# One stream of attention across eight images: second layer behind the next image's first unit, four single PSUM banks for the maxima

## The chip, the cores and the metric

The kernel runs on one core of a Trainium2 chip. A core has five engines with instruction queues of their own: TensorE (PE in the profile; its weight loads are PEld), VectorE (DVE), ScalarE (ACT), GpSimd (POOL) and SyncE (SP, which here only issues DMAs). Each engine takes its instructions in the order in which the program gives them; an instruction whose inputs are not ready holds up all that stand behind it on that engine. Matmul results land in PSUM, which has eight banks of 2 KB per partition (512 fp32 columns on 128 partitions). The metric is the device time of one execution in microseconds (us).

## What is computed

The input is eight images of 32 x 32 positions and 256 channels (1024 tokens of 256). Cut to what matters, the reference is

```python
x = x + L0_conv(group_norm(x))          # layer 0: 3x3 convolution and attention side by side
t = tokens(x)
t = t + L1_attn(layer_norm(t))          # layer 1: plain attention
t = t + L1_ffn(layer_norm(t))           # two experts per image
```

with, in layer 0,

```python
conv_out = conv3x3(x, conv_w) + conv_b                      # 192 channels
k, q, v = split(x @ qkv_w + qkv_b); q = q * DKH ** -0.5     # 64 each, 8 heads of 8
logits = q @ k.T + rel_w + rel_h                            # 1024 x 1024 for each head
attn = softmax(logits) @ v                                  # 64 channels
out = concat([conv_out, attn @ attn_w + attn_b])
```

where `rel_w` and `rel_h` are products of q with tables of relative positions. Layer 1 is attention with one head of 128 over the 1024 tokens (`softmax(Q @ K.T / sqrt(128)) @ V @ W_o + b_o`, plus its input). The feed-forward part chooses two of eight experts per image from the mean token, and stands behind all eight images.

## The kernel before

Layer 0's attention of an image is cut into four *units*. A unit is one half of the queries (512) and four of the eight heads. For a unit the kernel holds a tile `F` (queries together with the relative-position features, 128 partitions, for both halves of the keys) and a tile `KM` (keys together with 0/1 rows that pick the positions), so that one matmul of `F` with `KM` gives the whole logit. `KM` has one copy, used by the even units in heads 0 to 3 and by the odd ones in heads 4 to 7.

Each unit goes through two passes, because the maximum over the keys has to be known before the exponential:

- *score* (`Unit.score`): for 128 queries and one head, two matmuls of 512 keys into a PSUM tile of two banks (L610), and one DVE maximum over its 1024 columns (L617). 16 of these make a unit. PSUM holds two such tiles (`ps_lg`), and nearly all other small PSUM work goes through the same two.
- *fold* (`Unit.fold`): the 16 maxima are split into two fp32r parts, turned by four transposes (L628), copied to a row (L634), and written by four small DMAs on SP's queue into rows of `F` (L636), so that the next matmul gives the logit less its maximum.
- *weigh* (`Unit.weigh`): the transposed logit for 128 keys and one head, 512 columns (L646), and its exponential on ACT (L653). 32 of these make a unit.
- *gather* (`Unit.gather`): for each 128 keys, eight matmuls of the weights with the values (L661), four of them at a time side by side in the array. After the last, ACT copies the sum and *settle* turns and divides it.

The order of the work is written out by hand (`tc.manual_schedule()`); no planner moves anything. `first_layer` runs an image's four units in steps. A step `s` scores two heads of unit `s // 8` and weighs four heads of the unit that lies ten steps (`lead = NT + LAG`) behind:

```python
lead = NT + LAG
for s in range(units[0].scored // 2, NU * NT + lead + 1):
    u, j = divmod(s, NT)
    w, k = divmod(s - lead, NT)
```

So at first steps only score, then score and weigh, and the last ten only weigh. Between them `fill.send(us)` puts in other work: one step of a *chain* (generators that stop at each `yield`: `normalise` of the next image from step 12 on, `project`, `token_mean`), and `us` worth of *dense* work (the convolution's matmuls, L550, in pieces of estimated cost 0.36 us).

`normalise` transposes the next image (L339), takes group statistics (L349), makes q, k and v, writes the keys to DRAM, and combines the image on DVE (L433) and POOL (L436) into the six tiles `V` of the convolution. `queries` and `keys` load `F`'s source and `KM` (L490) by DMA, `features` makes the relative-position parts (L506) and writes them to DRAM, from where `Unit.__init__` loads `F` (L591, L595).

When an image's weighing has ended, `first_layer` issues `keys` of the next image, ends the second `project` half, and `second_layer` follows: for each 128 tokens two score matmuls (L846), one maximum over 1024 columns (L849), one exponential over 1024 columns (L852), transposes (L864), and for each 256 tokens the product with the values (L929) and with `W_o` (L940). Beside it run the pieces of `features` and the first scores of the next image's unit 0. `token_mean` stores the image and takes its mean for the expert choice.

## Time and profile before

| | us |
|---|---|
| median of three runs | 2888.73 (2887.54 to 2895.56) |
| profiled execution | 2892.55 |
| its span, first to last instruction | 2890.8 |
| PE busy | 2432.7 |
| DVE busy | 1408.4 |
| ACT busy | 975.7 |
| POOL busy | 369.8 |
| mean granted TensorE clock | 0.92 of full speed |

How to read it: the page gives busy time by engine over one execution, 40 slices of the span with busy tenths, the chain of work that ended last, and groups of equal instructions (line, engine, operation, output<-inputs, shapes, count | busy us, mean ns of one | idle time of the engine just before them and what ended it). A row of a table of windows is one stretch: its length, then for each engine busy us and the number of instructions, then the granted TensorE clock, the busy share of the 16 DMA engines and GB/s. A row of the timeline is start, length, engine, line, operation and tiles, with the idle time of the engine before it in brackets. SPq is SyncE's sequencer issuing DMAs.

In the span, image 2's second layer begins at 903.3 us, and image 3's at 1190.0 us; image 0's first score stands at 123.2, the last image's second layer runs from 2298.1 to 2344.5, and the feed-forward part follows.

### The profile page before, as it was taken

The page shows a single profiled execution, that of the slowest core. Times are in us where ns is not written, and L with a number is a line of the kernel's source. Part 1 is how long each engine was busy: PE and PEld are TensorE (multiplying, and loading weights), DVE is VectorE, ACT ScalarE, POOL GpSimd, SP SyncE. Part 2 cuts the span into 40 slices and gives each one's busy share as a digit, 9 for nine tenths or more (in the row PEclk, how much of TensorE's full clock was granted, in tenths as well). Part 3 has the DMA queues.
Part 4 walks back from the last instruction along what each step waited for, and adds up shares of the span by engine and source line. Part 5 has one row for each costly group of instructions (what it writes and reads, how often), then busy time and mean ns, then how long its engine had stood idle before and what let it go on. Part 6 is the DMA issues. An engine that isn't in the chain of part 4 may idle for free.

```text
span 2890.8 us, 28135 instructions
## 1 busy us (share of the span) xinstructions
PE 2432.7 (84%) x10731; PEld 1466.5 (51%) x10731; DVE 1408.4 (49%) x2525; ACT 975.7 (34%) x1717; POOL 369.8 (13%) x290
## 2 busy tenths in 40 slices
PE   4678878887898788878987888788889769999998
PEld 3544545455445544544454445544554346666665
DVE  6456356536643564366436644663467242332232
ACT  1035313531453145314531453145225422223222
POOL 3111102100211021102110211021100021111110
PEclk6789988998899899989998999899989979999999
DMA  3530343034213411441144114411421031112110
GB/s 94 128 76 18 76 105 64 22 78 104 53 31 84 102 40 31 87 103 37 31 87 102 37 31 97 92 38 34 112 59 31 1 106 58 59 59 73 58 51 22
DMA packets 81945, 185.94 MB, mean 64 GB/s; under 512 B 8546, under 2 KB 20715, under 8 KB 79507
## 3 DMA queue, kind: packets, MB, share of 16 engines
q1 hardware_dynamic: 79154, 182.05, 26.4%
q10 hardware_dynamic: 2656, 2.10, 0.3%
q8 instruction: 85, 1.39, 0.2%
q14 instruction: 50, 0.40, 0.1%
HBM read 112.15 MB, written 62.52 MB: 60 GB/s over the span
## 4 chain that ended last, share of the span: by engine, by line
PE 68%; DVE 20%; ACT 6%; issue 3%; DMA 2%; POOL 1%; SPq 1%; ACTq 0%; DVEq 0%; POOLq 0%
PE st L646 9%; PE po L661 8%; PE py L1214 8%; PE phd L1196 8%; DVE mx L617 7%; PE lg L610 6%; PE pc L550 5%; PE po L929 4%; PE lg L846 3%; PE pq L745 2%; ACT PT L653 2%; PE pmean L971 2%; DVE nm L849 2%; DVE V L433 2%; PE pk L386 2%
## 5 line engine op out<-in xcount | busy, mean ns | idle before, releaser
L653 ACT ACTIVATE PT<-st 128x512 f32<-128x512 f32 x1024 | 590.5, 597 | 492.1 <-PE st L646 444.9
L617 DVE TENSOR_REDUCE mx<-lg 128x1 f32<-128x1024 f32 x512 | 605.1, 1216 | 237.7 <-PE lg L610 235.1
L610 PE MATMUL lg<-KM,F 128*128 128x512 f32 x1024 | 379.7, 457 | 147.9 <-DVE mx L617 54.7
L646 PE MATMUL st<-F,KM 128*128 128x512 f32 x1024 | 470.2, 479 | 32.8 <-ACT PT L653 28.7
L646 PEld LDWEIGHTS st<-F,KM 128*128 128x128 f32 x1024 | 192.5, 197 | 340.0 <-ACT PT L653 258.4
L550 PE MATMUL pc<-convw,V 128*128 128x192 f32 x1152 | 296.5, 363 | 47.1 <-POOL V L436 29.2
L610 PEld LDWEIGHTS lg<-KM,F 128*128 128x128 f32 x1024 | 195.3, 206 | 244.1 <-DVE mx L617 92.1
L661 PE MATMUL po<-PT,vk 128*32 128x512 f32 x2048 | 292.4, 632 | 0.0
L550 PEld LDWEIGHTS pc<-convw,V 128*128 128x128 f32 x1152 | 216.4, 209 | 89.9 <-POOL V L436 32.7
L1214 PE MATMUL py<-w,hT 128*128 128x256 f32 x1024 | 237.3, 385 | 0.0
L1196 PE MATMUL phd<-n2T,w 128*128 128x512 f32 x512 | 223.2, 594 | 0.0
L1214 PEld LDWEIGHTS py<-w,hT 128*128 128x128 f32 x1024 | 189.9, 190 | 45.6 <-issue 22.4
L1221 DVE TENSOR_TENSOR r<-py,n 128x256 f32<-128x256 f32 x64 | 27.1, 424 | 311.2 <-PE py L1214 311.2
L846 PE MATMUL lg<-nqk 128*128 128x512 f32 x256 | 141.0, 679 | 24.1 <-ACT pr L852 24.1
L1196 PEld LDWEIGHTS phd<-n2T,w 128*128 128x128 f32 x512 | 97.0, 191 | 115.8 <-issue 108.9
L852 ACT ACTIVATE pr<-lg,nm 128x1024 f32<-128x1024 f32 x64 | 71.3, 1113 | 217.2 <-DVE nm L850 202.8
L733 POOL TENSOR_TENSOR T<-T,n 128x256 f32<-128x256 f32 x64 | 48.3, 773 | 717.8 <-DVE n L730 717.8
L567 DVE TENSOR_TENSOR ms<-mm 128x192 f32<-128x192 f32 x32 | 11.4, 357 | 239.5 <-ACT mm L565 239.5
L1203 ACT ACTIVATE hT<-phd,b1c 128x512 f32<-128x512 f32 x128 | 86.3, 686 | 97.6 <-PE phd L1196 97.4
L379 POOL TENSOR_TENSOR T<-T,l0b 128x2048 f32<-128x2048 f32 x8 | 36.2, 4527 | 643.8 <-PE tpx L339 643.8
L849 DVE TENSOR_REDUCE nm<-lg 128x1 f32<-128x1024 f32 x64 | 78.1, 1220 | 80.6 <-PE lg L846 80.6
L929 PE MATMUL po<-pt,v 128*128 128x256 f32 x512 | 115.9, 379 | 0.4 <-DVE pt L867 0.4
(246 smaller groups left out, 2525.0 us busy)
## 6 DMA issues: line engine op xcount, KB each, us to landing
F<-fd SPq DMA_DIRECT2D x64, 768.0 KB
fy<-rel SPq DMA_DIRECT2D x32, 512.0 KB
F<-fy SPq DMA_DIRECT2D x128, 128.0 KB
w<-in_L_ffn_W_dram SPq DMA_DIRECT2D x32, 512.0 KB
T<-in_x_dram SPq DMA_DIRECT2D x16, 512.0 KB
scr<-kqh SPq DMA_DIRECT2D x64, 128.0 KB
fd<-kqh SPq DMA_DIRECT2D x32, 256.0 KB
KM<-kd SPq DMA_DIRECT2D x32, 256.0 KB
```

The lines of the kernel that those rows point to most:

```text
L550: nc.tensor.matmul(pc[:, i], lhsT=V[j][:, kc, (16 * g + dy) * NQ : (16 * g + dy) * NQ + P], rhs=convw[:, j, dy * KC + kc], start=dy + kc == 0,
L610: nc.tensor.matmul(lg[:, a, :], lhsT=self.F[:, a, hl, i * P : (i + 1) * P], rhs=KM[:, self.g * HG + hl, a * 512 : (a + 1) * 512], start=Tr ...
L617: nc.vector.tensor_reduce(self.mx[:, i, hl : hl + 1], lg.rearrange("p a s -> p (a s)"), AX.X, ALU.max, negate=True)
L646: nc.tensor.matmul(st, lhsT=KM[:, self.g * HG + hl, j * P : (j + 1) * P], rhs=self.F[:, j // 4, hl, :], start=True, stop=True,)
L653: nc.scalar.activation(self.pts[j][:, hl, :], st, AF.Exp)
L661: nc.tensor.matmul(self.po[32 * hl : 32 * hl + 32, :], lhsT=vk[:, j, (self.g * HG + hl) * (DH + 1) : (self.g * HG + hl) * (DH + 1) + 32], ...
L846: nc.tensor.matmul(lg[:, h, :], lhsT=q, rhs=k[:, h * 512 : (h + 1) * 512], start=True, stop=True)
L849: nc.vector.tensor_reduce(nm, lg, AX.X, ALU.max, negate=True)
L929: nc.tensor.matmul(po[:, 0:IB], lhsT=sec.v[:, jc, :], rhs=pt[:, jc, :], start=jc == 0, stop=jc == NT - 1)
L1196: nc.tensor.matmul(phd, lhsT=ws[k][0][:, kc, f * P : (f + 1) * P], rhs=n2T[:, kc, q * 512 : (q + 1) * 512], start=kc == 0, stop=kc == KC - 1,)
L1203: nc.scalar.activation(hT[:, k * NF + f, :], phd, AF.Gelu, bias=b1c[:, f, k * B + b : k * B + b + 1])
L1214: nc.tensor.matmul(py, lhsT=hT[:, k * NF + f, j * P : (j + 1) * P], rhs=ws[k][1][:, f, :], start=False, stop=k == TOPK - 1 and f == NF - 1,)
```

## The change

The four parts of it:

1. `ps_lg` becomes four single banks instead of two pairs. A *score* is now one matmul of 512 keys and one DVE maximum over 512 columns, 32 to a unit; `fold` takes the smaller of the two negated halves first. The second layer's scores, maxima and exponentials go by halves too, and its value product uses a bank of this pool.
2. `first_layer` runs over 32 steps an image, without a lag: each step weighs four heads of its unit, and beside them scores the *next* unit, also across images (the next one of image b's unit 3 is image b+1's unit 0). Scores stand at places 3 to 27 of a unit's 32 weighing places, `fold` (DVE) at place 28, `fold_in` (transposes, row, DMAs) at place 30.
3. An image's second layer, with both halves of its projection, moves into the next image's run: `project` is chained during the next image's unit 0, and `second_layer` stands whole between the next image's units 0 and 1. The last image's follows at the end, alone.
4. All filling goes in smaller pieces and at every weighing place (`normalise`, `combine`, `features`, `project`), `features` and `queries` become part of the chain of `normalise`, the next image's tile is fetched at step 8, `keys` is loaded in two halves of four heads each, and `F` has three fixed places instead of a ring of three.

The diff, cut to its core ("..." marks what is left out):

```diff
-        ps_lg = ph.enter_context(tc.tile_pool(name="ps_lg", bufs=2, space=PSUM))
+        ps_lg = ph.enter_context(tc.tile_pool(name="ps_lg", bufs=4, space=PSUM))
...
-            return ps_lg.tile([P, 2, 512], FP, tag="lg", name=name)
+            return ps_lg.tile([P, 512], FP, tag="lg", name=name)
...
-        def f_tile(name, dt=FR):
-            return work.tile([P, 2, HG, 512], dt, tag="F", name=name, bufs=3)
+        def f_tile(name, place, dt=FR):
+            return work.tile([P, 2, HG, 512], dt, tag=f"F{place}", name=name)
...
             for kc in range(KC):
-                tp = turned(kc)
-                for q in range(2):
-                    nc.vector.bn_stats(st[:, kc, q, :], tp[:, q, :])
+                for g in range(2):
+                    nc.vector.bn_stats(st[:, kc, g, :], turned(kc, g))
+                    yield None
...
+            while b > 0 and (done[b - 1] < NT or not may_query.get(b)):
+                yield None
+            qs, qx = queries(b)
...
-            while b > 0 and done[b - 1] < NT:
-                yield None
             yield from combine(b, base)
-
+            yield from features(b, qs, qx)
+            yield None
+            yield None
+            yield None
+            units[b, 0] = Unit(b, 0)
+            yield None
...
-        def keys(b):
+        def keys(b, g):
+            hs = slice(g * HG, (g + 1) * HG)
             for i in range(4):
                 nc.sync.dma_start(
-                    out=KMb[8 * i : 8 * i + 8], in_=kds[b % 2][i % 2].rearrange("(d h) s -> d h s", h=NH)
+                    out=KMb[8 * i : 8 * i + 8, hs],
+                    in_=kds[b % 2][i % 2].rearrange("(d h) s -> d h s", h=NH)[:, hs],
                 )
...
-                self.F = f_tile("F")
+                self.F = f_tile("F", 2 if n == 3 else (b + n) % 2)
...
             def score(self):
 
-                i, hl = divmod(self.scored, HG)
+                n, a = divmod(self.scored, 2)
+                i, hl = divmod(n, HG)
                 self.scored += 1
                 lg = lg_tile("lg")
-                for a in range(2):
-                    nc.tensor.matmul(
...
+                nc.tensor.matmul(
+                    lg,
+                    lhsT=self.F[:, a, hl, i * P : (i + 1) * P],
+                    rhs=KM[:, self.g * HG + hl, a * 512 : (a + 1) * 512],
+                    start=True,
+                    stop=True,
                 )
+                nc.vector.tensor_reduce(self.mx[:, a, i, hl : hl + 1], lg, AX.X, ALU.max, negate=True)
 
             def fold(self):
 
+                assert self.scored == 32
+                m = self.mx[:, 0]
+                nc.vector.tensor_tensor(m, m, self.mx[:, 1], ALU.min)
...
+            def fold_in(self):
+
+                pm = lg_tile("pmx")
...
-        def first_layer(b, units):
...
-                if s == 12 and more:
-                    T[b + 1] = load_image(b + 1)
-                    fill.chains.append(normalise(b + 1))
...
+        def fetch(b):
+            T[b] = load_image(b)
+            for _ in range(4):
+                yield None
+
+        def pace(b, s, p):
+
+            if done.get(b, NT) < NT:
+                left, later = 4 * (15 - s) - p, 5.0 if s < NT else 0.0
+            else:
+                left, later = 4 * (32 - s) - p + 24, 5.0
+            return max(fill.owed - later, 0.0) / max(left, 1)
...
+        def first_layer(b):
+
             more = b + 1 < B
+            for s in range(NU * NT):
+                n, j = divmod(s, NT)
+                unit = units[b, n]
+                nxt = (b, n + 1) if n + 1 < NU else (b + 1, 0) if more else None
+                if s == 0:
+                    if b > 0:
+                        keys(b, 1)
+                elif s == NT:
+                    units[b, 2] = Unit(b, 2)
+                    if b > 0:
+                        while fill.chains:
+                            fill.send(0.4)
+                        second_layer(b - 1, sec, [units[b, 0].gather, lambda: settle(b, 0)], units[b, 2])
+                        fill.chains.append(token_mean(b - 1))
+                    else:
+                        units[b, 0].gather()
                         fill.send(0.4)
+                        settle(b, 0)
+                    if more:
+                        fill.chains.append(fetch(b + 1))
+                        fill.chains.append(normalise(b + 1))
+                elif s == NT + 1:
+                    units[b, 3] = Unit(b, 3)
+                elif s == 2 * NT:
+                    may_query[b + 1] = True
+                elif s == 3 * NT and more:
+                    keys(b + 1, 0)
+                    units[b + 1, 1] = Unit(b + 1, 1)
+                for p in range(HG):
+                    place = 4 * j + p
+                    unit.weigh(j, p)
+                    if nxt in units:
+                        u = units[nxt]
+                        while u.scored < min(32, (place - 3) * 4 // 3 + 1):
+                            u.score()
+                        if place == 28:
+                            u.fold()
+                        elif place == 30:
+                            u.fold_in()
+                    elif nxt is not None:
+                        assert place < 28
+                    if p == 1:
+                        if j > 0:
+                            unit.gather()
...
+                    if s == 1 and p == 0 and b > 0:
+                        sec = Second(b - 1)
+                        for half in range(2):
+                            fill.chains.append(project(b - 1, sec, half, (2, 4, 2)))
+                    fill.send(pace(b, s, p) * (0.6 if p == 1 else 1.13))
...
             def scores(self, blk, i, q, k, rs, scale):
-                lg = lg_tile("lg1")
+                lg = [lg_tile("lg1") for h in range(2)]
...
+                    nc.tensor.matmul(lg[h], lhsT=q, rhs=k[:, h * 512 : (h + 1) * 512], start=True, stop=True)
+                    nc.vector.tensor_reduce(nm[:, h : h + 1], lg[h], AX.X, ALU.max, negate=True)
...
-                    po = ps_po.tile([P, 512], FP, tag="po", name="po1")
+                    po = lg_tile("po1")
...
+            units[0, 1] = Unit(0, 1)
+            for g in range(NG):
+                keys(0, g)
+            for _ in range(32):
+                units[0, 0].score()
+                fill.send(0.2)
...
+            for b in range(B):
+                first_layer(b)
+            units[B - 1, NU - 1].gather()
+            settle(B - 1, NU - 1)
+            sec = Second(B - 1)
+            for half in range(2):
+                fill.chains.append(project(B - 1, sec, half, (1, 3, 1)))
+            while fill.chains:
                 fill.send(1.0)
...
+            second_layer(B - 1, sec, [], None)
             fill.chains.append(token_mean(B - 1))
             fill.finish()
```

## The prediction

> **What bounds the kernel now.** I read the page first: engine totals, the slices, the chain.
>
> ```profile
> PE 2432.7 (84%) x10731; PEld 1466.5 (51%) x10731; DVE 1408.4 (49%) x2525; ACT 975.7 (34%) x1717; POOL 369.8 (13%) x290
> ...
> PE   4678878887898788878987888788889769999998
> ...
> DVE  6456356536643564366436644663467242332232
> ...
> PEclk6789988998899899989998999899989979999999
> ...
> PE 68%; DVE 20%; ACT 6%; issue 3%; DMA 2%; POOL 1%; SPq 1%; ACTq 0%; DVEq 0%; POOLq 0%
> ```
>
> The chain lies on PE for 68% and on DVE for 20%. About 31 of the 40 slices are the two attention layers of eight images; the last stretch, the feed-forward part, is solid PE and not in the diff. Images repeat every 286.7 us, so I cut one period, 903.3 to 1190.0 us, where its work changes.
>
> ```profile
> core 0: us, PE busy (x) PEld busy (x) DVE busy (x) ACT busy (x) POOL busy (x), PEclk, DMA share, GB/s
> 903.30:969.60 66.30, 53.00 (x236) 37.81 (x236) 33.34 (x51) 19.08 (x35) 2.00 (x2) 0.92 0.54 126
> 969.60:1008.40 38.80, 28.96 (x101) 17.44 (x100) 24.73 (x49) 2.00 (x6) 0.00 (x0) 0.77 0.35 83
> 1008.40:1057.30 48.90, 44.00 (x221) 26.51 (x220) 29.89 (x41) 19.86 (x36) 7.09 (x3) 0.90 0.09 23
> 1057.30:1095.30 38.00, 31.36 (x150) 15.20 (x148) 28.48 (x36) 19.09 (x34) 8.01 (x10) 0.96 0.34 71
> 1095.30:1139.00 43.70, 38.06 (x185) 19.68 (x184) 25.74 (x40) 21.15 (x41) 6.37 (x6) 0.92 0.00 1
> 1139.00:1164.90 25.90, 23.43 (x120) 10.18 (x122) 0.63 (x3) 18.63 (x35) 5.04 (x3) 1.00 0.38 82
> 1164.90:1190.00 25.10, 19.63 (x110) 13.91 (x107) 9.53 (x30) 3.69 (x8) 5.92 (x6) 1.00 0.34 42
> ```
>
> The rows are: the second layer; scores with no weighing yet; weighing of units 0, 1, 2 beside scores; unit 3 weighed with no scores; the last projection. ACT idles in row 2 and DVE in row 6: that is what one stream could close. Busy PE includes pipeline latency, so I count PE work by the trace's distance between starts: 0.232 us for a 512-column fp32r matmul, 0.175 for a convolution piece, 0.12 for a gather matmul, 0.429 for 512 fp32 columns, 0.216 for 256, 0.11 to 0.14 for the small ones, 0.30 for the means. The rows hold 45.2, 20.3, 36.3, 25.4, 31.1, 19.0 and 17.3 us of it: 194.6, or 0.68 of the period. Row 2 is worst (0.52, clock 0.77).
>
> **The change, part by part.**
>
> *The second layer as a block.* The same matmuls, now without the relative-position pieces. For the last image, where nothing stands beside it, it took 46.4 us (2298.1 to 2344.5) for 37.6 us of work. It keeps one gather, one settle, eight half scores and some convolution, 5 us of work, partly in its gaps: 52 us against 66.3. Splitting its exponentials costs ACT 2 x (0.60 + 0.19) - (1.11 + 0.19) = 0.28 us a row block, 2.2 us an image, under PE's work.
>
> *The stream.* What remains for PE is 194.6 - 37.6 - 5 = 152 us an image. Row 3, the nearest mixture of weighing, scores and convolution, does 36.3 us in 48.9: 0.74. Its clock of 0.90 lost 4.9 us; without that it would be 0.82. I take the middle, 0.78: 152 / 0.78 = 195 us.
>
> *Halved reductions.* The widths from the groups:
>
> ```profile
> L617 DVE TENSOR_REDUCE mx<-lg 128x1 f32<-128x1024 f32 x512 | 605.1, 1216 | 237.7 <-PE lg L610 235.1
> ...
> L349 DVE BATCH_NORM_STATS2 gst<-tpx 128x6 f32<-128x512 f32 x32 | 20.9, 690 | 15.0 <-PE tpx L339 14.7
> ```
>
> A 512-wide PSUM read took 690 ns, so 512 x (2 x 0.690 - 1.216) = 84 us more DVE in all, 10.5 an image, and 1.3 more in the second layer. DVE then has about 137 us (152.3 in the period and 10.5, less some 26 in the second layer) in a 195 us stream, so I put it beside PE; without that cover it costs up to those 84. Four single banks give back some waits of row 4, where PE's scores waited for a bank behind the combination on V; I put that into the density. The Trainium skill, Perfetto Trace Analysis, section Optimizing Scalar/DVE Operations, gives some 125 ns of overhead per DVE operation on PSUM and advises larger operations on a saturated engine; by its figure the split would be an estimated 64 us, 20 less than by the row, and no other sum uses it.
>
> *Keys, moved onto the path.* Before, one load of KM follows the last weighing and the second layer hides it.
>
> ```profile
> 876.88 1.29 SPq L490 DMA_DIRECT2D KM<-kd  x4
> ...
> 881.00:889.00 8.00, 6.53 (x43) 5.60 (x42) 5.16 (x22) 0.41 (x2) 0.00 (x0) 1.00 0.49 57
> ```
>
> Its four transfers of eight 32 KB packets run one after another on half the DMA engines (share 0.49), 4.34 us each; the last landed 19.5 us after the first issue. Now each half is loaded when the unit that read it ends, and the next scores, three places later on in-order PE, read it. With 16 KB packets I halve the 17.4 us: 8.7 + 2.1 = 10.8 us. SP first issues the four maxima copies (2.5 us), so the load starts 0.85 us after the next unit's first weighing; three places take some 3 us. PE stands for 10.8 + 0.85 - 3 = 8.7 us, with all weighing, convolution and gathers behind it. After idle stretches the clock records show half clock for 6.8 us, partly still idle: 1.8 us more. So 10.5 us, twice an image, 14 in all: 147 us. From both sides: 0 if the packets shrink more than their size, 21 if halving them saves nothing. The Trainium skill, DMA: Bandwidth & Descriptors, section Rules for kernel authors, says that the slowest dimension sets the engines used, here 8 of 16, and advises 16 or more rows, which this split does not do. Were the engine count all that slowed these packets, the 8 KB packets' 0.312 us would make a half load an estimated 4.6 us and the stalls about 90 us less in all; the 32 KB row is the same transfer, so I keep to it.
>
> *Maxima, with the lag gone.* Before, weighing follows the scores by ten steps, two behind the fold. Now the fold's transposes come at place 30 of 32 and the next unit's weighing two places later.
>
> ```profile
> 1038.94 0.60 PE L628 MATMUL pmx<-ident,mh 128*8 128x128 f32 x4 [1.04 <-DVE mh L625]
> 1039.58 0.68 DVE L634 CAST mb<-pmx 8x512 fp32r<-8x512 f32 x1 [0.78 <-PE pmx L628]
> 1040.28 2.47 SPq L636 DMA_DIRECT2D F<-mb  x4
> ```
>
> The first of these landed at 1041.95, 3.0 us after the transposes began. PE has 1.5 us of work between: a stall of 1.5 us at the three boundaries without a second layer, 4.5 us an image; 0 if filling covers it, 5 each if the fourth copy counts.
>
> *Image load.* T is loaded behind a unit's F on SP's queue, as before (issues at 711.9 and 716.1), when its first transposes came 14 us later, at 730.6. Now they come four places, 6.5 us, after the issue, and T landed at about 729. So 6.5 us of PE stall and 1.5 of half clock: 8 us, seven times (0 to 10).
>
> *Projection* now shares DVE with reductions: PE's wait for its normalised rows (31.4 us in all before) stays, 4 us an image. *Features, F loads, value copies:* ten more SP issues an image at 0.3 to 0.6 us, and the same POOL copies; they run behind two steps or more of the stream, 12 us, against 10.5 us for an F load. If that cover is gone, an F load is worth up to 10 us.
>
> *Ends.* Before, image 0's first score came at 123.2. Now both F loads (last issue 121.6) precede the keys: 121.6 + 10.8, then 32 half scores at 0.75 alone, and 6 for fold and copies: the stream starts at 163. Image 0 has no projection (15.4 us of PE work), mean (5.3) or second layer, 131 us of work: 168 + 6 + 10.5 + 8 = 192.5. Image 7 has no next image (normalising 10.9, positions 7.1, scores 7.3, early convolution 14), 113 us: 145 + 3 + 10.5 + 4 + 52 = 214.5. Behind it stand both projections (19 each, from 2279.0 to 2298.1 before), a settle of 3, the second layer at 47 and the mean at 6: 95.
>
> *Sum.* A middle image is 195 + 4.5 + 21 + 8 + 4 + 52 = 284.5. 163 + 192.5 + 6 x 284.5 + 214.5 + 95 = 2372. Before, that point lies near 2350, so 541 us follow: a span of 2913. The profiled run took 1.75 more than its span and 3.8 more than the median of the three runs: 2911, say **2912 us**, +0.8%. What merging closes, some 40 us an image, is eaten by 21 + 8 + 4.5 + 4 of new waits and by the longer ends.
>
> **The rivals.**
>
> *Denser stream (faster).* Each 0.01 of density is 195 / 78 x 7.4 images = 18.5 us. The sign turns above 0.79. Clean steps speak for it: four weighs, four score halves and eight gather matmuls take 3.30 us for 2.8 us of work, 0.85. At 0.82 to 0.85 it ends at 2780 to 2840. Against: half clock follows every stall of 3 us in this trace.
>
> *Keys hidden.* If the scores find KM landed, 147 us go: 2765. In-order PE speaks against it.
>
> *DVE becomes the bound.* 32 half reductions in 24 places take 22 us plus some 11 of other DVE work there. If PE runs in lockstep, density falls to row 4's 0.67 to 0.71: 3040 to 3110. Row 4 speaks for it, the four banks against.
>
> *No gain in the second layer.* If it stays at 66 us, as its waits on maxima and exponentials suggest, 14 x 7 = 98 more: 3010.
>
> **How the numbers follow.** Forecast 48%, alone 2850 to 2980; denser 18%; keys hidden 8%; DVE 18%; second layer 8%. Runs spread by 8 us, so 0.3% is about what can be told from no change. Of the forecast, 0.18 falls below 2880 and 0.15 within; with the rivals, faster is 0.09 + 0.17 + 0.07 = 0.33, same 0.08, slower 0.59. The range of 2790 to 3050 leaves out the hidden keys and the far end of DVE.
>
> **What would show it.** The chain of waits should name KM<-kd before a score 14 times, about 8 us each, with half clock behind; T before the transposes seven times; F<-mb before weighing at 1 to 2 us. The second layer should take 50 to 55 us, a middle image 275 to 295. PE standing on DVE maxima means the third rival; no waits on KM, or a period below 270, make the prediction wrong.

## The result, and the profile after

The changed kernel takes 2912.43 us (median of four, 2911.99 to 2914.22) against 2888.14: a ratio of 1.008, 95% interval 1.0062 to 1.0097. It is slower by 0.8%, and the predicted time was 2912. The profiled execution took 2911.99 us, its span 2910.2. On the page after: engine totals, slices of PE, DVE and the granted clock, and the chain.

```profile
PE 2414.5 (83%) x10731; PEld 1516.7 (52%) x10731; DVE 1479.7 (51%) x3213; ACT 991.0 (34%) x1877; POOL 372.9 (13%) x290
...
PE   3579788968887887788879878987898769999998
...
DVE  5356465636654665565556545654565352233232
...
PEclk6787889889988997899789968986999879999999
...
PE 64%; DVE 17%; DMA 13%; SPq 2%; ACT 2%; issue 1%; POOL 1%; DVEq 0%; ACTq 0%
```

In the middle DVE's slices are mostly 5 and 6 now, where before they swung between 3 and 6 or 7: the stream does spread its work. But DMA, 2% of the chain before, is 13% of it. One period, cut at the same places of the work (unit 0; second layer; units 1, 2, 3):

```profile
core 0: us, PE busy (x) PEld busy (x) DVE busy (x) ACT busy (x) POOL busy (x), PEclk, DMA share, GB/s
925.80:992.10 66.30, 50.47 (x246) 29.77 (x247) 38.61 (x82) 22.49 (x44) 13.39 (x13) 0.87 0.05 9
992.10:1042.70 50.60, 48.31 (x229) 34.88 (x228) 31.46 (x71) 18.93 (x48) 0.00 (x0) 1.00 0.22 42
1042.70:1093.80 51.10, 39.92 (x198) 21.58 (x196) 28.23 (x70) 19.46 (x38) 7.06 (x3) 0.93 0.41 93
1093.80:1162.50 68.70, 54.31 (x261) 36.49 (x261) 37.24 (x67) 24.44 (x46) 14.39 (x14) 0.76 0.51 123
1162.50:1209.60 47.10, 38.06 (x187) 23.76 (x187) 24.29 (x45) 19.83 (x34) 0.00 (x0) 0.88 0.40 57
```

The period is 283.8 us long, 286.7 before. The second layer takes 50.6 instead of 66.3, at full clock. By distance between starts PE has 46.8 us of work in that row (0.92 of it) and 148.5 in the other four (0.64 of 233.2). Unit 2 is the worst row: 38.9 us of work in 68.7, clock 0.76. PE's own waits (engine, line, releaser: us in total, times, longest) say what fills the holes:

```profile
PE lg L623 <- DMA KM<-kd: 122.3, 15, 30.4
PE st L664 <- DMA F<-mb: 99.2, 26, 11.4
PEld lg L623 <- DVE mx L630: 40.8, 78, 1.8
...
PE tpx L342 <- DMA T<-in_x_dram: 28.2, 6, 5.4
...
PE lg L623 <- DVE mx L630: 13.9, 17, 1.5
```

PE's waits for keys, maxima and the image come to 249.7 us. The wait for a bank behind a maximum has fallen to 40.8, from these of the kernel before:

```profile
PEld lg L610 <- DVE mx L617: 92.1, 85, 2.1
PE lg L610 <- DVE mx L617: 54.7, 74, 1.8
```

A PEld row and a PE row can show one wait twice, since the weight load and its matmul stand for the same bank: all 17 of PE's waits above lie inside PEld's, and so do all 74 of the kernel before. So PEld's figure is the wait, and 92.1 - 40.8 = 51 us of it are gone, while three DMA waits have come in. Of the keys' 122.3 us, 30.4 stand once, ahead of image 0's first score; the other fourteen average 91.9 / 14 = 6.6. One of them on the timeline (start, length, engine, line, operation and tiles, idle time before it):

```profile
923.94 2.48 SPq L654 DMA_DIRECT2D F<-mb  x4
...
925.78 0.47 PE L664 MATMUL st<-F,KM 128*128 128x512 f32 x1 [2.03 <-DMA F<-mb]
...
926.51 1.38 SPq L500 DMA_DIRECT2D KM<-kd  x4
...
935.60 0.77 PE L623 MATMUL lg<-KM,F 128*128 128x512 f32 x1 [7.02 <-DMA KM<-kd]
```

The copies of the maxima hold PE for 2.03 us, and the keys, issued 0.73 us after the unit's first weighing, hold it for 7.02 with the rest of the weighing behind. The score then runs 0.77 instead of 0.39 us, at half clock. The costliest boundary is another, from unit 2 to unit 3:

```profile
1147.89 1.94 SPq L604 DMA_DIRECT2D F<-fd  x2
1149.55 0.60 PE L646 MATMUL pmx<-ident,mh 128*8 128x128 f32 x4
1149.88 2.78 SPq L608 DMA_DIRECT2D F<-fy  x4
1150.19 0.68 DVE L652 CAST mb<-pmx 8x512 fp32r<-8x512 f32 x1 [0.67 <-PE pmx L646]
1152.76 9.66 SPq L654 DMA_DIRECT2D F<-mb  x4
1162.47 0.77 PE L664 MATMUL st<-F,KM 128*128 128x512 f32 x1 [11.44 <-DMA F<-mb]
```

The next image's first unit has just put its F load (six transfers, 2048 KB by the page) on SP's queue. The row of maxima is ready at 1150.87, but SP spends 9.66 us on the four 8 KB copies that follow, against 2.48 above, and PE waits 11.44. The semaphore events of the trace tell more. The first weighing needs the first copy alone (head 0). SP had issued it by 1153.37, but it landed at 1162.34, 9.6 us after its issue began, when nearly all of F had landed; the one issued at 923.94 landed in 1.7. PE starts 0.13 us after this landing. SP's long issue is another matter: the third and fourth copies use the completion semaphores (107 and 108) of F's two 768 KB transfers again, and SP issues them 0.07 us after these have landed, at 1156.21 and 1161.91.

### The profile page after: what moved, and what is told of

Read it like the earlier page. It is cut to its first block, busy times and chain, and to the rows that moved or that the text cites. A ratio compares the mean times of both kernels' runs of the same rounds, so it can differ in the third digit from the quotient of the medians.

```text
span 2910.2 us, 29034 instructions
## 1 busy us (share of the span) xinstructions
PE 2414.5 (83%) x10731; PEld 1516.7 (52%) x10731; DVE 1479.7 (51%) x3213; ACT 991.0 (34%) x1877; POOL 372.9 (13%) x290
## 4 chain that ended last, share of the span: by engine, by line
PE 64%; DVE 17%; DMA 13%; SPq 2%; ACT 2%; issue 1%; POOL 1%; DVEq 0%; ACTq 0%
PE py L1253 8%; PE phd L1235 8%; DVE mx L630 7%; PE st L664 7%; PE po L680 6%; PE lg L623 6%; PE pc L563 5%; DMA KM<-kd 5%; PE po L969 4%; PE lg L891 3%; PE prel L512 3%; DMA T<-in_x_dram 2%; PE pq L768 2%; DMA F<-fd 2%; DMA F<-fy 2%; DVE V L443 2%
## 5 line engine op out<-in xcount | busy, mean ns | idle before, releaser
L630 DVE TENSOR_REDUCE mx<-lg 128x1 f32<-128x512 f32 x1024 | 659.6, 683 | 525.1 <-PE lg L623 519.8
L664 PE MATMUL st<-F,KM 128*128 128x512 f32 x1024 | 549.1, 543 | 140.4 <-DMA F<-mb 99.2
L623 PE MATMUL lg<-KM,F 128*128 128x512 f32 x1024 | 416.0, 441 | 147.5 <-DMA KM<-kd 122.3
L664 PEld LDWEIGHTS st<-F,KM 128*128 128x128 f32 x1024 | 212.1, 210 | 324.2 <-ACT PT L671 172.6
L563 PE MATMUL pc<-convw,V 128*128 128x192 f32 x1152 | 316.9, 366 | 20.5 <-POOL V L446 12.8
L896 ACT ACTIVATE pr<-lg,nm 128x512 f32<-128x512 f32 x128 | 86.8, 683 | 127.6 <-DVE nm L893 127.4
L891 PE MATMUL lg<-nqk 128*128 128x512 f32 x256 | 120.3, 593 | 0.0
L892 DVE TENSOR_REDUCE nm<-lg 128x1 f32<-128x512 f32 x128 | 86.6, 688 | 59.8 <-PE lg L891 59.8
L969 PEld LDWEIGHTS po<-pt,v 128*128 128x128 f32 x512 | 94.7, 190 | 19.8 <-DVE pt L918 8.3
L680 PEld LDWEIGHTS po<-PT,vk 128*32 128x32 f32 x2048 | 42.7, 113 | 98.1 <-issue 90.3
```

The source lines that it names most:

```text
L563: nc.tensor.matmul(pc[:, i], lhsT=V[j][:, kc, (16 * g + dy) * NQ : (16 * g + dy) * NQ + P], rhs=convw[:, j, dy * KC + kc], start=dy + kc == 0,
L623: nc.tensor.matmul(lg, lhsT=self.F[:, a, hl, i * P : (i + 1) * P], rhs=KM[:, self.g * HG + hl, a * 512 : (a + 1) * 512], start=True, stop= ...
L630: nc.vector.tensor_reduce(self.mx[:, a, i, hl : hl + 1], lg, AX.X, ALU.max, negate=True)
L664: nc.tensor.matmul(st, lhsT=KM[:, self.g * HG + hl, j * P : (j + 1) * P], rhs=self.F[:, j // 4, hl, :], start=True, stop=True,)
L680: nc.tensor.matmul(self.po[32 * hl : 32 * hl + 32, :], lhsT=vk[:, j, (self.g * HG + hl) * (DH + 1) : (self.g * HG + hl) * (DH + 1) + 32], ...
L891: nc.tensor.matmul(lg[h], lhsT=q, rhs=k[:, h * 512 : (h + 1) * 512], start=True, stop=True)
```

## The experiments

Each is compared with the kernel before, run on the same chip; the changed kernel's own ratio is 1.008. Differences "from the changed kernel" are between medians taken on different chips. The kernel before had medians of 2888.1 to 2896.0 us on these chips, so such a difference is good to some 8 us.

**1. keys_hidden.** Units go through both halves of the queries for heads 0 to 3 first, then for heads 4 to 7, so that each half of KM is free two units before it is needed again.

```diff
-                self.half, self.g = divmod(n, NG)
+                self.g, self.half = divmod(n, NG)
...
                 elif s == 2 * NT:
                     may_query[b + 1] = True
+                    if more:
+                        keys(b + 1, 0)
                 elif s == 3 * NT and more:
-                    keys(b + 1, 0)
```

> An image's units run as two query halves of heads 0-3, then two of heads 4-7, so each half of KM is free for a whole unit before it is read again; nothing else changes. In the changed kernel PE waits for KM 14 times in the stream, 92 us in all (7.4 to 7.9 at step 0, 4.7 to 6.4 at step 24), and every such wait is followed by about 6.8 us of half clock. Theory (the exposed load of the keys is paid in full): these waits go and take some 2 us of half clock each with them, 92 to 125 us less, 2790 to 2820 us. Rival (PE would stand then for DVE's maxima, or for another transfer): less than 30 us, 2880 to 2915 us, with new waits on mx or F in the scores' row.

Measured: 2828.41 us (2821.47 to 2842.17), ratio 0.979 (0.9753 to 0.9826): 84 us below the changed kernel, and below the kernel before. Its waits on PE:

```profile
PE st L664 <- DMA F<-mb: 106.3, 26, 11.5
PEld lg L623 <- DVE mx L630: 63.5, 57, 9.4
PE lg L623 <- DVE mx L630: 43.3, 10, 9.0
...
PE lg L623 <- DMA KM<-kd: 28.8, 1, 28.8
```

All fourteen waits in the stream are gone; what is left is image 0's first. The keys are the main cause, but 91.9 us of waits with their half clock gave 84, not the 92 to 125 expected: the waits for a maximum grew from 40.8 to 63.5 us (all ten of PE's lie inside PEld's). A quarter of the freed standing time reappears there. The rival named this wait, but DVE's load of maxima is not behind it. Five of these waits, 5.6 to 9.0 us long on PE and 38.5 us together on PEld, make more than the whole rise, and each looks like this one:

```profile
1327.39 1.38 SPq L500 DMA_DIRECT2D KM<-kd  x4
1328.81 10.40 SPq L480 DMA_DIRECT2D scr<-kqh  x8
...
1342.43 3.69 POOL L492 CAST scr<-scr 128x1024 fp32r<-128x1024 f32 x2 [20.41 <-DMA fd<-kqh]
...
1348.76 1.79 DVE L443 SCALAR_TENSOR_TENSOR V<-V,V 128x256 f32<-128x256 f32 x2 [7.35 <-POOL V L446]
...
1351.20 0.80 PE L623 MATMUL lg<-KM,F 128*128 128x512 f32 x1 [9.01 <-DVE mx L630]
```

The key load now stands on SP's queue ahead of the next image's query transfers (`scr`), whose issue takes 10.40 us where it took 5.02 in the changed kernel. POOL waits for them (the profile puts this wait down to the transfer issued next), DVE waits in its combination of `V` for POOL, and the maxima behind that on DVE keep PE from its bank. In the changed kernel POOL waited 9.8 to 14.9 us at that place, and DVE not at all.

**2. keys_16_rows.** The keys stay where the change put them; each load becomes two transfers of 16 rows instead of four of eight.

```diff
-            for i in range(4):
+            for i in range(2):
                 nc.sync.dma_start(
-                    out=KMb[8 * i : 8 * i + 8, hs],
-                    in_=kds[b % 2][i % 2].rearrange("(d h) s -> d h s", h=NH)[:, hs],
+                    out=KMb[16 * i : 16 * i + 16, hs],
+                    in_=kds[b % 2].rearrange("l (d h) s -> (l d) h s", h=NH)[:, hs],
```

> The half load of the keys goes as two transfers of 16 rows instead of four of 8, same bytes, same place. Theory (the transfers run one after another, and each is limited by the 8 rows that it writes): two transfers of 2.2 us instead of four, 4.4 us less for each of 14 waits, 60 us, and some half clock: 2835 to 2855 us, KM waits of 1 to 3.5 us. Rival (the bytes or the source limit it): the waits stay at 5 to 8 us and the time at 2905 to 2915 us.

Measured: 2855.89 us, ratio 0.987 (0.9847 to 0.9892), 56.5 below the changed kernel. The keys' waits of the profiled run (2835.69 us, 18 below the next of its five runs) are these; the 29.2 and the 29.5 are one wait, ahead of image 0's first score:

```profile
PE lg L623 <- DMA KM<-kd: 38.3, 4, 29.2
PEld lg L623 <- DMA KM<-kd: 29.5, 1, 29.5
```

By the gaps before scores (the profile puts some of them down to issue) those at an image's unit 3 shrink to 0.4 to 1.5 us (4.7 to 6.4 in the changed kernel); at an image's start a wait of 3.0 to 4.6 us stands where 7 to 8 stood. The packets show why. All are 16 KB in both kernels. Their median length was 1.66 us in the load shown above (up to 2.12 in others of that kernel) and 1.89 here, but up to 16 of them go at once instead of eight, and the last packet ended 5.0 us after the load's first issue (893.76 to 898.76) instead of 8.2 (926.51 to 934.72). This agrees with the Trainium skill's rule (DMA: Bandwidth & Descriptors, Rules for kernel authors) that the slowest dimension sets the number of engines (it advises a multiple of 16 there); the prediction named it, and the change did not follow it.

**3. maxima_on_act.** The copies of the maxima are issued from ACT's queue instead of SP's.

```diff
                 for h in range(HG):
-                    nc.sync.dma_start(
+                    nc.scalar.dma_start(
                         out=self.Fb[R_M : R_M + 33 : 32, :, h],
```

> The four copies of the maxima row are issued from ACT's queue instead of SP's. In the changed kernel the weighing of unit 3 waits 5.8 to 11.4 us for them, the others 2.0 to 2.5; at unit 3 SP issued them for 9.7 us behind the F load of the next image's first unit. Theory (the copies stand behind that load in SP's rings): unit 3's wait falls to 2 to 3 us, some 45 us less with 10 to 20 us of half clock: 2850 to 2870 us. Rival (the DMA engines themselves are full, or the wait is the copies' own latency): no wait falls by more than 2 us, 2895 to 2915 us.

Measured: 2921.98 us, ratio 1.0115 (1.0079 to 1.015), 9.6 above the changed kernel. The theory falls. Unit 3's wait did shrink to 2.1 to 6.9 us, but at an image's start it went from 2.0 to between 6.4 and 9.3, and the total on PE rose from 99.2 to 122.7. The keys' fourteen waits became seven of 10.3 to 11.5 us, 75.7 together instead of 91.9. A boundary between images on the timeline:

```profile
1213.28 1.29 SPq L500 DMA_DIRECT2D KM<-kd  x4
1213.77 2.20 ACTq L654 DMA_DIRECT2D F<-mb  x4
...
1222.84 0.76 PE L664 MATMUL st<-F,KM 128*128 128x512 f32 x1 [9.26 <-DMA F<-mb]
```

SP's order had kept the keys behind the copies. With two queues the keys go first, and the copies' first packet starts at 1218.82, 5 us after its issue, between the last of the keys' packets. The Trainium skill (Trainium Kernel Development and Optimization, Key Constraints) says that DMAs of all queues share the same engines, and that a second issuer saves only issue time; this run agrees, and costs a little more.

**4. image_before_F.** Unit 3's F load is issued one step later, so that the next image's load no longer stands behind it.

```diff
-                elif s == NT + 1:
+                elif s == NT + 2:
                     units[b, 3] = Unit(b, 3)
```

> The F load of unit 3 is issued at step 10 instead of 9, so that the image load goes ahead of it on SP's queue. Theory (the image stands behind 2 MB of F): PE's waits for T, 5.2 us six times, go with some 2 us of half clock each: 30 to 45 us less, 2868 to 2883 us. Rival (the image's own latency is the wait, or F comes late for the scores at step 16): 2900 us or more, and in the second case a new wait on F at the scores.

Measured: 2882.67 us (median of ten), ratio 0.9958 (0.994 to 0.9976), 29.7 below the changed kernel, as expected. Of PE's 28.2 us of waits on T 0.2 is left, so they cost their length and hardly more.

**5. fold_earlier.** Scores are packed closer, and the fold stands three places earlier.

```diff
-                        while u.scored < min(32, (place - 3) * 4 // 3 + 1):
+                        while u.scored < min(32, (place - 3) * 3 // 2 + 1):
...
-                        if place == 28:
+                        if place == 25:
                             u.fold()
-                        elif place == 30:
+                        elif place == 27:
```

> The next unit's 32 half scores stand at places 3 to 24 instead of 3 to 27, the fold at 25 and its transposes, row and copies at 27. In the changed kernel weighing waits 2.0 to 2.5 us for the copies at some 19 boundaries and 5.8 to 11.4 us at unit 3's seven. Theory (the copies' 3 us of latency stands bare because only two places cover it): the short waits go and unit 3's fall by some 4 us, 70 us less with up to 20 us of half clock: 2825 to 2850 us. Rival (scores at 1.5 a place make DVE the bound there, and PE waits for banks instead): 2885 to 2915 us, with PE waits on mx up by 30 us or more.

Measured: 2905.11 us (median of ten), ratio 1.0043 (1.0026 to 1.0061), only 7 below. PE's wait on the copies falls from 99.2 to 92.4 us: at an image's start it is gone, but unit 3's grow (5.8 to 11.4 us before, 8.6 to 12.7 now). They end about when the F load ends, whenever the fold begins: one first copy, issued at 1164.96, landed at 1174.22. The waits on maxima rise from 40.8 to 52.2 us. The theory fell. The rival's time held, but not its 30 us of waits on maxima.

**6. narrow_maxima.** Each maximum reads 256 columns instead of 512.

```diff
-                nc.vector.tensor_reduce(self.mx[:, a, i, hl : hl + 1], lg, AX.X, ALU.max, negate=True)
+                nc.vector.tensor_reduce(self.mx[:, a, i, hl : hl + 1], lg[:, 0:256], AX.X, ALU.max, negate=True)
```

> Left out: every maximum of a half score reads 256 of its 512 columns, so the maxima are over half the keys. DVE has some 1024 x 0.267 = 273 us less work, and nothing else changes. Theory (DVE is not what limits the stream; PE with its waits on transfers is): 2880 to 2912 us. Rival (DVE bounds the scores' places): 100 us less or more, 2810 us or below.

Measured: 2836.17 us, ratio 0.9812 (0.9783 to 0.984), 76 below. The group of maxima, in the changed kernel and then here (busy us, mean ns):

```profile
L630 DVE TENSOR_REDUCE mx<-lg 128x1 f32<-128x512 f32 x1024 | 659.6, 683 | 525.1 <-PE lg L623 519.8
```

```profile
L630 DVE TENSOR_REDUCE mx<-lg 128x1 f32<-128x256 f32 x1024 | 401.2, 418 | 637.7 <-PE lg L623 634.1
```

258 us less in this group bring 76: 0.29 of it was bare. DVE is neither fully covered, as the theory had it, nor the bound.

**7. before_halved_maxima.** The kernel before, with each maximum split in two of 512 columns. To make room, `mh` has one buffer instead of two.

```diff
-                nc.vector.tensor_reduce(
-                    self.mx[:, i, hl : hl + 1], lg.rearrange("p a s -> p (a s)"), AX.X, ALU.max, negate=True
-                )
+                for a in range(2):
+                    nc.vector.tensor_reduce(self.mx[:, a, i, hl : hl + 1], lg[:, a, :], AX.X, ALU.max, negate=True)
```

> The kernel before, with each maximum over 1024 columns taken as two of 512 and one minimum a unit; banks, order and all else as before. DVE has 512 x (2 x 0.683 - 1.216) = 77 us more. Theory (the maxima stand bare where nothing is weighed beside them, 14 to 30 of an image's 64): 17 to 36 us more than before, 2905 to 2925 us. Rivals: hidden everywhere, 2885 to 2895 us; paid in full, 2960 us or more.

Measured: 2915.21 us, ratio 1.0081 (1.0064 to 1.0098), 24 above the before of its chip (2891.0). A half takes 681 ns against 1216 for the whole, which by count makes 512 x 0.146 = 75 us more. But neighbours on DVE overlap: 1024 x 0.681 = 697 us of these maxima keep it busy for 637.7. Its busy time rose by 45.5 (1408.4 to 1453.9), against which 24 us of time, about half, were paid. So the split alone costs this kernel as much as the whole change does. The single `mh` was not run by itself.

**8. F_load_sooner.** Six stops of the chain that ends in unit 0's F load are left out, to move that load away from the fold.

```diff
-                if j % 2:
+                if j == 3:
                     yield None
...
             yield from features(b, qs, qx)
-            yield None
-            yield None
-            yield None
             units[b, 0] = Unit(b, 0)
```

> Six of the stops in the next image's chain are left out (three in front of its values, three behind its features), so that its first unit's F load is issued some six places sooner and has gone when unit 3's maxima copies are issued. Theory (those copies stand behind that load): unit 3's wait of 5.8 to 11.4 us falls to 2 to 3, some 45 us less and 10 to 20 us of half clock: 2850 to 2870 us. Rival (the load waits for the features' own writes and comes no sooner): 2900 to 2912 us.

Measured: 2930.37 us, ratio 1.0134 (1.0106 to 1.0162), 18 above the changed kernel. Both theories missed. On the timeline the load has moved 2 us away from the copies, no more:

```profile
1154.37 1.71 SPq L601 DMA_DIRECT2D F<-fd  x2
1156.12 2.83 SPq L605 DMA_DIRECT2D F<-fy  x4
...
1160.99 7.40 SPq L651 DMA_DIRECT2D F<-mb  x4
```

SP's queue is the limit: the writes of the features stand ahead of the load on it until 1154.19. Unit 3's wait is still 6.3 to 8.1 us. Images 2 to 6 take 290 us each, 25 us more in all than in the changed kernel. Half clock covers 78.5 us in each of them, 24 us more in all, which costs at most 12. Over the whole execution half clock is the same, 671 us in both, so the clock alone does not make the 18 us; where the rest lies stays open.

**9. keys_and_image.** Experiments 1, 2 and 4 together.

```diff
-            for i in range(4):
+            for i in range(2):
...
-                self.half, self.g = divmod(n, NG)
+                self.g, self.half = divmod(n, NG)
...
-                elif s == NT + 1:
+                elif s == NT + 2:
                     units[b, 3] = Unit(b, 3)
                 elif s == 2 * NT:
                     may_query[b + 1] = True
+                    if more:
+                        keys(b + 1, 0)
                 elif s == 3 * NT and more:
-                    keys(b + 1, 0)
```

> The three edits on loads together: units in the order that frees half of KM early, key loads of 16 rows, the image's load ahead of F's. Alone they were worth 84 (keys hidden), 56 (16 rows, on waits that are gone once the keys are hidden) and 30 us (image). Theory (each wait is paid in full and on its own): 84 + 30, some 2800 us, at most 10 less for 16 rows. Rival (the time freed goes to DVE's maxima, whose waits on PE rose from 55 to 107 us when the keys were hidden): 2815 to 2830 us.

Measured: 2763.36 us (2761.04 to 2772.21), ratio 0.9558 (0.9534 to 0.9583): 149 below the changed kernel and 4.4% below the kernel before, more than the 84 + 30 = 114 of experiments 1 and 4. The same period as above, 259.3 us long, cut at the same places:

```profile
core 0: us, PE busy (x) PEld busy (x) DVE busy (x) ACT busy (x) POOL busy (x), PEclk, DMA share, GB/s
886.50:944.80 58.30, 49.50 (x246) 29.49 (x247) 38.62 (x82) 22.66 (x44) 13.37 (x13) 0.91 0.07 11
944.80:995.40 50.60, 48.32 (x229) 34.88 (x228) 31.48 (x71) 18.91 (x48) 0.00 (x0) 1.00 0.21 42
995.40:1039.40 44.00, 38.02 (x198) 20.10 (x196) 27.81 (x69) 19.47 (x38) 7.05 (x3) 1.00 0.42 108
1039.40:1106.60 67.20, 51.64 (x260) 33.05 (x260) 40.35 (x67) 24.29 (x46) 14.60 (x14) 0.81 0.55 133
1106.60:1145.80 39.20, 36.44 (x187) 22.69 (x187) 24.20 (x45) 19.83 (x34) 0.00 (x0) 0.93 0.28 55
```

Unit 0 is 8.0 us shorter (keys at the image's start), unit 1 7.1 (T, and no half clock), unit 3 7.9 (keys at its start); the second layer is the same, and unit 2, with its copies behind an F load, lost only 1.5. Its waits on copies and maxima:

```profile
PE st L664 <- DMA F<-mb: 108.1, 28, 11.5
PEld lg L623 <- DVE mx L630: 44.9, 69, 3.4
...
PE lg L623 <- DVE mx L630: 21.2, 19, 3.0
```

The waits on maxima are 44.9 us, not the 63.5 of experiment 1: the five long ones are gone, none is over 3.4 (the 55 and 107 of the expectation add PE's and PEld's rows). The trace says by what. The keys' two transfers of 16 rows leave SP sooner, the `scr` transfers behind them take 6.10 us to issue instead of 10.40, and DVE no longer waits for POOL. The period has 41 us of half clock (shares short of 1.00 in the clock column: 5.2 + 12.8 + 2.7 = 20.7 us lost, twice that at half clock), the whole execution 514, against 582 in experiment 1 and 671 in the changed kernel. That is where the extra 35 us show. The two added edits were not run apart.

**10. loads_and_maxima.** Number 9, the copies on ACT's queue, and `keys(b, 1)` one step later.

```diff
-                    nc.sync.dma_start(
+                    nc.scalar.dma_start(
                         out=self.Fb[R_M : R_M + 33 : 32, :, h],
...
-                if s == 0:
+                if s == 1:
                     if b > 0:
                         keys(b, 1)
```

> The same three edits, with the maxima copies on ACT's queue and the odd heads' keys loaded at step 1 instead of 0. On ACT's queue alone, the copies passed the F load's issue but met the keys' packets, and nothing was won. Theory (with the keys out of the way, unit 3's wait of 6 to 11 us falls to 2 to 4, and the others stay at 2): 30 to 50 us below the kernel with the three edits. Rival (the copies' packets wait on the DMA engines behind F, whatever the queue): within 15 us of it.

Measured: 2787.37 us, ratio 0.9642 (0.9601 to 0.9682), 24 above number 9. Unit 3's wait fell to between 1.8 and 6.7, but at the next image's start it rose from 2.0 to between 5.2 and 6.2 us, with total waits on the copies at 99.3 us against 108.1. The edit did not take the keys out of the way there:

```profile
1150.88 0.80 SPq L500 DMA_DIRECT2D KM<-kd  x2
1151.36 4.04 ACTq L654 DMA_DIRECT2D F<-mb  x4
...
1157.07 0.76 PE L664 MATMUL st<-F,KM 128*128 128x512 f32 x1 [5.90 <-DMA F<-mb]
```

With the copies off its queue, SP reaches the key load as soon as that half of KM is free, whatever step it is written at, and at all seven image starts it issues the keys 0.1 to 0.5 us ahead of the copies, as in experiment 3. Half clock rose from 514 to 569 us, worth at most 27; why is not shown.

**11. keys_hidden_narrow.** Experiment 1 with the maxima of experiment 6.

```diff
-                self.half, self.g = divmod(n, NG)
+                self.g, self.half = divmod(n, NG)
...
-                nc.vector.tensor_reduce(self.mx[:, a, i, hl : hl + 1], lg, AX.X, ALU.max, negate=True)
+                nc.vector.tensor_reduce(self.mx[:, a, i, hl : hl + 1], lg[:, 0:256], AX.X, ALU.max, negate=True)
```

> Keys hidden as before, and every maximum of a half score reads 256 of its 512 columns (left out: half the keys of each maximum). With the keys' waits in, this took 76 us off. Theory (what was freed went partly to DVE, which now holds PE 107 us on banks): 90 to 130 us below the kernel with the keys hidden alone, 2700 to 2740 us. Rival (DVE's share is the same with or without those waits): 70 to 85 us, 2745 to 2760 us.

Measured: 2759.59 us, ratio 0.9553 (0.951 to 0.9595): 69 below experiment 1, where narrowing the maxima of the changed kernel gave 76. DVE's bare share is the same with and without the keys' waits, so these were not hiding DVE time; the theory of a bound that comes forward fell. Narrower maxima leave four waits of 4.4 to 8.6 us for a bank, again with DVE waiting for POOL: the "107 us on banks" of the expectation was 63.5, and most of that was not DVE's own work.

**12. keys_first.** Number 9, with image 0's keys ahead of its second F load.

```diff
-            units[0, 1] = Unit(0, 1)
             for g in range(NG):
                 keys(0, g)
+            units[0, 1] = Unit(0, 1)
```

> The three load edits, and at the start the keys are issued ahead of the second F load of image 0, not behind it. In the kernel with the three edits the first score waits 30.7 us for KM, which SP issues at 117.6 us; with this order SP is free for it at 107.3. Theory (the keys stand behind that load): the first score and all behind it come 10 to 13 us sooner, 2750 to 2755 us. Rival (the first F load or the features set the first score, or the second F load then comes late for the stream): within 4 us of 2763 us.

Measured: the first wait on keys fell from 30.7 to 18.7 us and the first weighing came at 156.7 instead of 160.4. Five of its runs lie between 2736.03 and 2766.21, further apart than the 4 to 13 us in question, and a sixth took 2792.40. The middle of the five is 2762.4 us, which is number 9's time; the ratio, on another chip, is 0.9513 (0.9481 to 0.9544), which is lower. Single images took 259 us with 41 to 44 us of half clock or 267 with 61 to 65. What this edit is worth stays open.

## Why the prediction was right, and where it was not

The time and the sign came out as predicted, and the mechanism was the one named: what merging closes is eaten by DMA waits that the new order puts on PE, and by longer ends. Without the waits named below, the stream takes 233.2 - 34.2 = 199.0 us against 286.7 - 66.3 = 220.4 of the same work before, and the second layer 15.7 less: 37 us an image, where the prediction said some 40. Term by term for image 3:

| term | predicted us | measured us |
|---|---|---|
| second layer | 52 | 50.6 |
| keys, two waits | 17.4 | 7.0 + 6.3 = 13.3 |
| image load T | 6.5 | 5.2 |
| maxima, three waits | 4.5 | 2.0 + 2.3 + 11.4 = 15.7 |
| rest of the stream | 195 + 4 + 5.1 of half clock = 204.1 | 199.0 |
| period | 284.5 | 283.8 |

- *Second layer as a block*: held. It was denser than the last image's alone (0.92 against 0.81): the pieces placed in it filled its gaps.
- *Stream*: held in sum. 148.5 us of work in 199.0 is 0.75; the prediction's 152 in 204.1 is the same. Its 0.78 was too high only where it counted lost clock separately.
- *Keys*: the mechanism held, fourteen times; each wait was 6.6 us on average instead of 8.7. The term mis-sized is the load, 9.1 us from its issue to the score (926.51 to 935.60) instead of 10.8: its packets took 7.2 from first to last (927.49 to 934.72), where half of 17.4 was priced, and 1.9 stood around them instead of 2.1. Experiment 1 shows that the whole is worth 84 us, where 147 was priced. A quarter of the time set free goes to other waits for a bank, which come from the key load's new place and not from the maxima.
- *Keys by engine count*: the prediction set the estimate of 4.6 us for a half load aside, and rightly: the 9.1 measured is nearer to its 10.8. What it did not price is a load of 16 rows; that took 56.5 us off, with packets of about the same length.
- *Maxima*: the ordinary boundaries were 2.0 to 2.5 us (predicted 1.5). The step that failed is the one that priced all three alike, and left F loads under two steps of cover: at unit 3 the copies stand behind the next image's F load, and the first of them lands only when nearly all of F has. The load itself was covered; what stood behind it was not. That one wait of 11.4 outweighs all that keys and T were overpriced by. Another queue and a shorter chain made it smaller but not the time, and an earlier fold made it longer (experiments 3, 10, 8 and 5).
- *Image load*: held six times instead of seven, mostly 5.2 us for 6.5 (image 0 stands for unit 2's F load at that place instead). Experiment 4 gives 29.7 us, against the seven times 8 priced: the half clock behind it was not to be seen in the time.
- *Halved reductions*: 84 us came from durations times count, which count overlaps twice; alone the split is 45.5 us of busy time (experiment 7), to which the 64 us that the prediction left aside is nearer, and the whole change adds 71.3 (1408.4 to 1479.7). Put beside PE at nothing, that failed in part: by experiment 6 some 0.29 of it is bare, an estimated 21 us. It lies inside the stream's density, with the 51 us of waits for a bank that went; which part of these the four banks took was not run by itself.
- *Half clock*: predicted behind every stall. The clock column gives 0.13, 0.07, 0.24 and 0.12 of four rows, 34 us lost in the period; the five rows of before that fell short lost 24. Over the whole execution half clock covers 671 us, against 463 before. How much of the 0.8% is the clock's cannot be told apart from the waits: part of it falls on idle PE, and the runs that took the keys' or the image's waits away also had less of it (582 us in experiment 1, 561 in 2, 658 in 4).
- *Ends*: the stream began at 155.7 (163) and image 0 took 200.0 (192.5), 8.5 of it a wait on unit 2's F load, which has no second layer to hide behind; image 7 took 210.0 (214.5) and what follows 92 (95). The six periods between, from image 1's first weighing to image 7's, took 1712.7 us against 1713.1 before. So the middle images together neither won nor lost (image 3 is one of the better ones), and the 19 us by which the profiled span grew lie at the ends.

So the total was closer than its terms: keys 4 too high, maxima 11 too low, rest 5 too high an image. That these nearly cancel, and that the time came out within 1 us, is luck. *Denser stream* and *DVE becomes the bound* did not come; *keys hidden* is what experiment 1 makes of it, and there 2828, not 2765, is the time. *No gain in the second layer* is out by the windows.

## What to carry to other kernels

When stages are merged into one stream, list every operand with a single buffer that the old seams reloaded, and every queue that was empty there: here a key load of 512 KB, an image load and four 8 KB copies cost a middle image about what a better-packed PE gained, and the ends made the kernel slower. The remedy was mostly in the order: going through the heads so that each key half is free two units early, moving one load a step, and loading the keys by 16 rows turned +0.8% into -4.4%. A load moved off the path can still hold up what is issued behind it, as the keys did to the queries in experiment 1. Small copies that a stage waits for landed in 1.7 us with nothing ahead of them and in 9.6 behind a large load; no run here put them ahead of it, and changing the queue alone did not. And before adding up rows of waits, see whether two of them are one wait.

## What the runs showed of the hardware

- Of four 8 KB copies the first landed 1.7 us after its issue with nothing ahead of it, and 9.6 behind a load of 2048 KB on the same queue. SP took 2.48 and 9.66 us to issue the four; in the second case it waited until two transfers of that load had landed, since the third and fourth copies use their completion semaphores again. From ACT's queue their first packets started 5 us after the issue, among packets of a load that SP had issued 0.5 us earlier.
- A transfer's rows set how many packets go at once: the last of 32 packets of 16 KB ended 8.2 us after the issue with eight rows to a transfer and 5.0 with sixteen, while the median packet took 1.7 us in the first load and 1.9 in the second.
- Half clock comes in pieces of 3.41 us: the images' totals of 41.0, 47.8, 68.3 and 75.1 us are 12, 14, 20 and 22 of them. The Trainium skill (TensorE: Matmul & The Clock Gate, What's actually happening) gives a free-running window of that length. Equal images of one run took 259 or 267 us with 41 to 44 or 61 to 65 us of it (experiment 12). Its five runs spread by 1.1%, with a mean granted clock of 0.91 in the two quickest and 0.90 in the others, so with runs that spread like this a change of less than 1% can be the clock's.
- PE reads 83 to 86% busy in all these runs, while the time moved by 6%.
